# Layer 0 of a four-layer graph network: one excursion from the weighing per tile, and its weights fetched during the first product

## The chip, the core and the metric

The kernel runs on one core of a Trainium2 chip. The core has a matmul engine (TensorE, PE in the profile; its weight loads are listed as PEld), three elementwise engines (VectorE or DVE, ScalarE or ACT, GpSimd or POOL) and queues that issue DMA transfers (SyncE, SP, issues nearly all of them here). The engines run side by side, each in the order of its own instruction stream, and wait for each other through semaphores. The metric is the device time of one execution in microseconds; lower is better.

## The reference

Four graph layers, each followed by a residual sum and a layer norm. x is 8 x 2048 x 64 in float32, adj is 2048 x 2048, sparse and row-normalised. Layer 0 is the one that the change touches, with the beginning of layer 1:

```python
# layer 0: node-wise weights from a 16-wide embedding, three graph terms
w = einsum('nd,dkio->nkio', embedding, weight)      # d = 16, k = 3
b = einsum('nd,do->no', embedding, bias)
As = [I, A, 2 * A @ A - I]
x_g = einsum('knm,bmc->bnkc', stack(As), x)
out = einsum('bnki,nkio->bno', x_g, w) + b
x = layernorm(x + out)
# layer 1, first lines
h = x @ W
s = leaky_relu(h @ a_node, 0.2)
alpha = softmax(where(H.T > 0, s, NEG))             # 64 hyperedges
agg = einsum('ben,bnf->bef', alpha, h)
beta = sigmoid(h @ a_gn + agg @ a_ge)
industry = einsum('nm,bmf->bnf', adj / deg, x @ W_ind)
...
```

Layers 1 (the rest), 2 and 3 use adj again as a matrix product each.

## The kernel before, in words

The 2048 nodes are cut into 16 tiles of 128; j counts them. A tile's data are 128 nodes by 512 columns (8 batches times 64 channels). adj is turned into a mask of zeros and ones and a factor for each row (s1), so that products with it can be done as two exact halves in a fast matmul type: every operand of such a product is split into a high and a low part (y_hi, y_lo).

**First product** (`first_product`, lines 444 to 544). y1 = A x for all tiles, in 32 pieces of the adjacency, with the membership lists of layer 1 prepared between the matmuls (`prepare`, `memberships`). Its accumulators come from a pool of seven (`ps_acc`).

**Layer 0's loop** (`layer0`, lines 987 to 1403). The loop at line 1337 goes over j from 0 to 16. For each tile it does eight *weighings* (`weigh`, g = 0 to 7). A weighing multiplies the three terms of the tile (x, y1 and y2, transposed) with a slice of the layer's weights on PE, on two halves of 64 rows, into a buffer pp (`ps_p`, two buffers of two banks); VectorE then drains it with four operations that scale by the embedding and add to r (L1141). All other work is placed by hand between the weighings, by the value of g: `normed` (layer norm of tile j-1, in three steps), `first_terms` (transposing y1 of tile j+1, its bias through a small matmul bp, and starting r with x plus bias), `project` (h = x W and x W_ind of tile j-2), `product` (y2 of tile j+1, 32 matmuls), `to_features` (transposing the normed tile), `compare` (checks that the mask times its factor is adj), `scaled` (mask times factor and the column sums for the degrees, on GpSimd), `mask` (mask of tile j+2), `scores` (eight matmuls with `wa` for the attention logits, exponential), `low_part` and `gather` (the weighted sum over hyperedges, `aggp`), `second_term` (transposing y2) and `degrees`.

PE leaves the weighing four times in a tile: after g = 2 (`first_terms`), 3 (`project`, `product`, `to_features`), 6 (`second_term`, `scores`, `gather`) and 7 (`degrees`); each of these lines stands below. `program_order` (line 212) fixes the order of PE, VectorE, ScalarE and GpSimd to that of the program text. SP is not fixed: a scheduler places its transfers by priority and by what they wait for. The buffers of the loop are tiles of one large pool (`own`), shared in turn by the table `homes`, and small ones in `l0s`, whose storage was used before by the lists' preparation. `load_w0` is called after the first product; `load_weights` (layer 1's small weights, and the sums for `wa`) in the first round of the loop.

Of the kernel before, what the change touches and what calls it, by code (L numbers as in the profile page):

```python
# [18 lines left out]
P = 128  # L19
# [43 lines left out]
def kernel(  # L63
# [170 lines left out]
    def load_w0(pool):  # L234
        w_sb = pool.tile([P, K, D * C], F32, tag="w", name="w0_sb")
        for h in range(2):
            nc.sync.dma_start(w_sb[h * 64:(h + 1) * 64], w0)
        emb_sb = pool.tile([P, NT, D], F32, tag="emb", name="emb_sb")
        nc.sync.dma_start(emb_sb, emb.rearrange("(t p) d -> p t d", p=P))
        bias_sb = pool.tile([D, C], F32, tag="bias", name="bias0_sb")  # L240
        nc.sync.dma_start(bias_sb, bias0)
        return w_sb, emb_sb, bias_sb
# [201 lines left out]
    def first_product(own, pre, rawp, mskp, y_hi, y_lo, prepare, after):  # L444

        x_hi, x_lo = buffer(own, 0, "x_hi"), buffer(own, 1, "x_lo")
        with tc.tile_pool(name="acc0", bufs=7, space=PSUM) as ps_acc, tc.tile_pool(
# [18 lines left out]

            steps = prepare(ps_s)
# [37 lines left out]
            with program_order():  # L505
# [5 lines left out]
                for n, (q, i, kk, h) in enumerate(pieces):  # L511
                    begin(n + 2)
                    if i + h == 0:
                        accs[q] = [
                            ps_acc.tile([P, BC], F32, tag="acc", name=f"y1p_{4 * q + jj}")
                            for jj in range(4)
                        ]
                    m = m_of.pop(n)
# [468 lines left out]
    def layer0(  # L987
        own, l0s, rawp, mskp, ps_acc, ps_tr, ps_p, w_sb, emb_sb, bias_sb, bad, deg, y_hi, y_lo,
        layer1s, load_weights, late_weights, begun,
# [4 lines left out]
        h_sb, wb, wa, vecs, av_sb, pm, es, hgr, aggp, rden, early = layer1s  # L994
        (raws, msk), terms, resid, norm, srow = begun, {}, {}, {}, {}
        x1s, xTs, hps, hss, mds = {}, {}, {}, {}, {}

        homes = {"xT": (0, 1, 2), "xs": (3, 4), "hs": (5,), "hsf": (15,), "y1T": (6, 7), "r": (8, 9),
# [15 lines left out]
        def load_x(j):  # L1014
            ncols = slice(j * P, (j + 1) * P)
            xT = tile("xT", f"xT_{j}", (P, NP, P))
            nc.sync.dma_start(xT, xt[:, :, ncols])
            et = tile("et", f"et_{j}", (D, P))
            nc.sync.dma_start(et, embt[:, ncols])
            xs = tile("xs", f"xs_{j}")  # L1020
            nc.sync.dma_start(xs, xn[ncols, :])
            terms[j] = {"x": xT, "et": et, "xs": xs}
# [29 lines left out]

        def first_terms(j):

            tr = ps_tr.tile([P, NP, P], F32, tag="tr", name=f"try1_{j}")
            if j > 1:
                y1 = tile("y1", f"y1_{j}", bufs=1)
                nc.gpsimd.tensor_tensor(y1, y_hi[:, j, :], y_lo[:, j, :], ALU.add)
            for pr in range(NP):
                pc = slice(pr * P, (pr + 1) * P)  # L1060
                if j > 1:
                    transpose(tr[:, pr, :], y1[:, pc])
                    continue
# [9 lines left out]
            bp = ps_tr.tile([P, QW], F32, tag="tr", name=f"bp_{j}")  # L1073
            nc.tensor.matmul(bp[:, 0:C], terms[j]["et"], bias_sb, start=True, stop=True)
            bn = tile("bn", f"bn_{j}", (P, C))
            nc.scalar.copy(bn, bp[:, 0:C])
            r = tile("r", f"r0_{j}")
            for bq in range(2):
                nc.gpsimd.tensor_tensor(  # L1079
                    r[:, 4 * bq * C:4 * (bq + 1) * C]  # L1080
                    .rearrange("p (h l c) -> p h l c", h=2, l=2),
                    swapped(terms[j]["xs"], bq),
                    bn.rearrange("p (h l c) -> p h l c", h=1, l=1).to_broadcast([P, 2, 2, C]),
                    ALU.add,
                )
            resid[j] = r
# [58 lines left out]
        def normed(j, step):  # L1145
            r = resid[j]
            if step == 0:
                s = tile("s", f"s_l0_{j}", (P, B))
# [7 lines left out]
            elif step == 1:  # L1156
                var = tile("var", f"var_l0_{j}", (P, B))
# [8 lines left out]
                std = tile("std", f"std_l0_{j}", (P, B))  # L1166
# [27 lines left out]
        def scores(j):  # L1194
            sp = ps_tr.tile([P, NP, 2, 2], F32, tag="tr", name=f"sgp_{j}")
            for pr in range(NP):
                nc.tensor.matmul(
                    sp[:, pr].rearrange("p i h -> p (i h)"), xTs[j][:, pr, :],
                    wa.rearrange("p i h -> p (i h)"), start=True, stop=True,
                )  # L1200
            sg = tile("sg", f"sg_{j}", (P, NP, 2))
            nc.scalar.copy(sg, sp[:, :, 0, :])
            nc.scalar.copy(hgr[:, j, 0, :].rearrange("p (r h) -> p r h", h=2), sp[:, :, 1, :])
            ej = es[:, j, :]
            nc.vector.scalar_tensor_tensor(
                ej.rearrange("p (r h) -> p r h", h=2), sg, 0.2, sg, op0=ALU.mult, op1=ALU.max
            )
            nc.vector.tensor_scalar(ej, ej, TOP, None, op0=ALU.min)
            nc.scalar.activation(ej, ej, AF.Exp)

        def project(j, h_first=False):

            mm = ps_p.tile([P, 2, 2, 4 * C], F32, tag="pp", name=f"hp_{j}")
            mm = mm.rearrange("p h l (m x) -> p h (l m) x", m=2)
            for pr in range(NP):
                for h in range(2):
                    rs = slice(h * 64, (h + 1) * 64)
                    nc.tensor.matmul(
                        mm[:, h, pr, :], xTs[j][rs, pr, :], wb[rs], start=True, stop=True
                    )  # L1220
            if j not in mds:
                md = tile("md", f"md_{j}", (P, 2, E))
                nc.gpsimd.tensor_copy(r_(md), pm[:, j, :].unsqueeze(1).to_broadcast([P, 2, E]))
                mds[j] = md.rearrange("p h e -> p (h e)")

            def by_half(t):
                return t.rearrange("p (r h c) -> p h r c", h=2, c=C)


            stay = j >= len(kept_i)  # L1230
            if stay:
                hi, lo = y_hi[:, j, :], y_lo[:, j, :]
            else:
                hi, lo = (tile(k, f"{k}_{j}", bufs=1) for k in ("ihi", "ilo"))
# [6 lines left out]
            if not stay:  # L1241
                for t, kept_part in zip((hi, lo), kept_i[j]):
# [8 lines left out]
            hss[j] = tile("hs", f"hs_hi_{j}"), hs  # L1251
            nc.scalar.copy(r_(hss[j][0]), hs)

        def low_part(j):
            if j < NT - 1:
                hi, hs = hss[j]

                lo = tile("x1", f"hs_lo_{j}", bufs=1)
                nc.gpsimd.tensor_tensor(r_(lo), hs, hi, ALU.subtract)
                hss[j] = hi, lo  # L1260
# [63 lines left out]
        load_x(0)  # L1324
        load_adj(1)
        load_x(1)
        with program_order():
            for j in range(2):
                for h in range(2):
                    mask(j, h)  # L1330
            first_terms(0)
            scaled(0, 0)
            scaled(0, 1)
            for _ in product(0):
                pass
            second_term(0)
            for j in range(NT + 1):
                first = j == 0
                if not first:
                    when(j + 2, load_adj)  # L1340
                when(j + 2, load_x)
                for g in range(8):
                    when(j, weigh, g)
                    if g == 0:
                        if j == NT:
                            spread()
                        when(j - 1, normed, 0)
                        if first:
                            compare(0, 0)
                            compare(0, 1)  # L1350
                            load_adj(2)
                            load_weights()
                        if j == 2:
                            late_weights()
                    elif g == 1:
                        when(j - 1, normed, 1)
                        if j == NT:
                            denp.append(
                                ps_p.tile([P, 2, 2, 4 * C], F32, tag="pp", name="denp")[:, 0, 0, 0:B]
                            )  # L1360
                            denominators(0, NT - 1)
                            early.extend(industry_early())
                            early.pop(0)(5)
                        if first:
                            degrees(0)
                        when(j + 1, scaled, 0)
                    elif g == 2:
                        when(j - 1, normed, 2)
                        when(j + 1, first_terms)
                    elif g == 3:  # L1370
                        when(j - 2, project)
                        if j + 1 < NT:
                            for _ in product(j + 1):
                                pass
                        when(j - 1, to_features)
                        when(j + 1, compare, 0)
                        when(j + 1, scaled, 1)
                        if j == NT - 2:
                            for t in range(len(kept_i)):
                                for y, kept_part in zip((y_hi, y_lo), kept_i[t]):  # L1380
                                    nc.sync.dma_start(y[:, t, :], kept_part)
                        when(j + 2, mask, 0)
                        when(j + 2, mask, 1)
                    elif g == 5:
                        when(j + 1, compare, 1)
                        when(j - 2, low_part)
                        if j:
                            next(flags, None)
                    elif g == 6:
                        when(j + 1, second_term)  # L1390
# [815 lines left out]
```

## Time and profile before

| | us |
|---|---|
| three runs, median | 1308.96 (1307.51 to 1308.96) |
| the profiled execution | 1308.88 |
| its span, first to last instruction | 1307.5 |
| first product, to its last matmul | 0 to 134.97 |
| joint: to the first weighing of tile 1 | 134.97 to 194.16 |
| tiles 1 to 14 | 194.16 to 662.49 |
| tile 15 | 662.49 to 689.16 |
| tail, to the last gather's end | 689.16 to 708.2 |
| the rest: layers 1, 2 and 3 | to 1307.5 |

The inner borders are read from PE's timeline. A profile is one execution recorded by the hardware. Its page gives the busy time of each engine, the span in 40 slices, the DMA queues, the chain of work that ended last, and the costliest groups of instructions; further views give the timeline of an engine, the waits, and busy times in chosen stretches. In a timeline the columns are start, duration, engine, line, operation, output and inputs, shapes and count; in brackets stands the idle time before an instruction and what ended it. A matmul of full float32 appears as two passes, so a count of x4 means two matmuls. Matmuls are pipelined and overlap, so on PE the distance between starts is the real cost, not the duration.

### The profile page before, as it was taken

What the parts mean: (1) busy time and instruction counts of PE and PEld (TensorE: products, weight loads), DVE (VectorE), ACT (ScalarE), POOL (GpSimd) and SP (SyncE); (2) the same over time, 40 slices, a digit from 0 to 9 for tenths busy, and PEclk for the clock granted to TensorE, in tenths of its full rate; (3) what the DMA queues carried; (4) which work ended last, traced back from release to release, by engine and by line L of the source; (5) the groups of instructions that cost most, each with busy time, mean ns of one, the idle gap of its engine ahead of it and who ended that gap; (6) DMA issues with size and microseconds to landing.
All of it is one profiled execution on the core that took longest, in us unless ns stands there. A gap on an engine that the chain in (4) does not pass through costs nothing. (4 is left out here: it accounts for less than half of the span.)

```text
span 1307.5 us, 20046 instructions
## 1 busy us (share of the span) xinstructions
PE 1250.4 (96%) x7724; PEld 1005.3 (77%) x7724; DVE 887.6 (68%) x1597; ACT 378.0 (29%) x852; POOL 512.2 (39%) x419
## 2 busy tenths in 40 slices
PE   9999789999999999999998599999998899999996
PEld 8887568888888888888886377777766788888885
DVE  5555368888887777778674567777774666655544
ACT  3000101222222222222222356666665521111111
POOL 1000354555555555555411568888872600000000
PEclk9999889999999999999998599999998999999998
DMA  8889532333332333332352212222220233334551
GB/s 285 253 234 182 162 116 93 108 104 103 107 102 97 108 108 108 108 108 81 121 179 97 80 65 97 97 98 97 81 97 1 82 112 129 107 119 153 184 177 67
DMA packets 100951, 157.22 MB, mean 120 GB/s; under 512 B 12912, under 2 KB 64496, under 8 KB 94832
## 3 DMA queue, kind: packets, MB, share of 16 engines
q1 hardware_dynamic: 98368, 151.65, 35.7%
q10 hardware_dynamic: 2304, 4.20, 0.8%
q8 instruction: 63, 1.03, 0.3%
q0 software_dynamic: 176, 0.02, 0.1%
q14 instruction: 40, 0.33, 0.1%
HBM read 118.08 MB, written 37.76 MB: 119 GB/s over the span
## 5 line engine op out<-in xcount | busy, mean ns | idle before, releaser
L1141 DVE SCALAR_TENSOR_TENSOR r<-pp,emb_sb,r 128x256 f32<-128x256 f32 x512 | 247.3, 483 | 109.1 <-PE pp L1130 94.0
L1130 PE MATMUL pp<-w_sb,xT 64*128 64x256 f32 x1024 | 161.6, 392 | 6.5 <-DVE r L1141 6.5
L1130 PE MATMUL pp<-w_sb,y1T 64*128 64x256 f32 x1024 | 154.1, 377 | 0.0
L1130 PE MATMUL pp<-w_sb,y2T 64*128 64x256 f32 x1024 | 154.1, 377 | 0.0
L1079 POOL TENSOR_TENSOR r<-xs,bn 128x256 f32<-128x256 f32 x32 | 22.8, 732 | 244.6 <-issue 216.8
L1130 PEld LDWEIGHTS pp<-w_sb,xT 64*128 64x128 f32 x1024 | 95.0, 187 | 24.6 <-issue 9.6
L1130 PEld LDWEIGHTS pp<-w_sb,y1T 64*128 64x128 f32 x1024 | 100.3, 188 | 11.0
L1130 PEld LDWEIGHTS pp<-w_sb,y2T 64*128 64x128 f32 x1024 | 100.1, 188 | 10.9
L1093 PE MATMUL y2p<-y_hi,msk 128*128 128x512 f32 x256 | 103.7, 405 | 0.0
L523 PE MATMUL y1p<-x_hi,m 128*128 128x512 f32 x256 | 103.0, 402 | 0.1
L1093 PE MATMUL y2p<-y_lo,msk 128*128 128x512 f32 x256 | 101.9, 398 | 0.0
L1468 PE MATMUL ind<-y_hi,mj_l 128*128 128x512 f32 x240 | 101.7, 424 | 0.0
L523 PE MATMUL y1p<-x_lo,m 128*128 128x512 f32 x256 | 101.0, 395 | 0.0
L1468 PE MATMUL a<-v_hi,mj_l 128*128 128x512 f32 x256 | 100.1, 392 | 0.0
L1468 PE MATMUL a<-v_lo,mj_l 128*128 128x512 f32 x256 | 100.0, 391 | 0.0
L1468 PE MATMUL a<-y_lo,mj_l 128*128 128x512 f32 x240 | 95.1, 396 | 0.0
L1468 PE MATMUL a<-y_hi,mj_l 128*128 128x512 f32 x240 | 94.9, 395 | 0.0
L1468 PE MATMUL ind<-y_lo,mj_l 128*128 128x512 f32 x240 | 94.6, 394 | 0.0
L1032 POOL TENSOR_TENSOR ms<-msk,srow 128x1024 f32<-128x1024 f32 x32 | 90.3, 2821 | 10.0 <-DVE ms L1048 5.7
L770 POOL TENSOR_TENSOR ez<-ez,coef 128x1024 f32<-128x1024 f32 x32 | 69.9, 2184 | 56.2 <-DVE ez L768 54.3
L440 DVE TENSOR_SCALAR msk<-adj 128x1024 fp32r<-128x1024 f32 x32 | 61.9, 1971 | 1.1 <-DMA adj<-in_at 1.1
L745 DVE TENSOR_TENSOR gp<-gp,rest 128x1024 f32<-128x1024 f32 (+1 forms) x32 | 30.9, 966 | 45.3 <-PE gp L738 45.0
(289 smaller groups left out, 2455.5 us busy)
## 6 DMA issues: line engine op xcount, KB each, us to landing
mj_l<-mask SPq DMA_DIRECT2D x46, 1024.0 KB, 4.9
adj<-in_at SPq DMA_DIRECT2D x64, 256.0 KB, 3.9
mask<-msk SPq DMA_DIRECT2D x32, 512.0 KB, 4.6
raw<-in_at SPq DMA_DIRECT2D x31, 512.0 KB, 5.2
oh<-oh SPq DMA_DIRECT2D x32, 128.0 KB, 3.9
xT<-in_xt SPq DMA_DIRECT2D x16, 256.0 KB, 3.0
xs<-in_xn SPq DMA_DIRECT2D x16, 256.0 KB, 2.9
kept<-x SPq DMA_DIRECT2D x16, 256.0 KB, 2.0
```

The source lines that it names most:

```text
L440: nc.vector.tensor_scalar(r_(m), raw, 0.0, None, op0=ALU.is_gt)
L523: nc.tensor.matmul(accs[q][jj], r_(m[:, t, jj * P:(jj + 1) * P]), r_(part[:, mt, :]), start=i + h + t == 0 and part is x_hi, stop=i == 3 a ...
L745: nc.vector.tensor_tensor(by_b(gp[:, 0:n]), by_b(gp[:, 0:n]), per_b(rest, 2 * i, n), ALU.mult)
L770: nc.gpsimd.tensor_tensor(by_b(ez), by_b(ez), per_b(coef, 2 * i, 2), ALU.mult)
L1032: nc.gpsimd.tensor_tensor(ms, m, srow[j].unsqueeze(1).to_broadcast([P, 8, P]), ALU.mult)
L1079: nc.gpsimd.tensor_tensor(r[:, 4 * bq * C:4 * (bq + 1) * C] .rearrange("p (h l c) -> p h l c", h=2, l=2), swapped(terms[j]["xs"], bq), bn. ...
L1093: nc.tensor.matmul(acc, r_(msk[j, mt // 8][:, mt % 8, :]), r_(part[:, mt, :]), start=mt == 0 and part is y_hi, stop=mt == NT - 1 and part ...
L1130: nc.tensor.matmul(pp[:, h, pl, :], terms[j][name][rs, 2 * bq + pl], w_sb[rs, k, dq * 4 * C:(dq + 1) * 4 * C], start=k == 0, stop=k == K - 1,)
L1141: nc.vector.scalar_tensor_tensor(rb, ppv[:, :, dd, :], emb_sb[:, j, d:d + 1], rb, op0=ALU.mult, op1=ALU.add)
L1468: nc.tensor.matmul(acc, r_(a[:, mt, :]), r_(part[:, mt, :]), start=mt == 0 and part is hi, stop=mt == NT - 1 and part is lo,)
```

## The change

Layer 0's loop is put in another order, and some of its pieces are cut differently.

- PE leaves the weighing once in a tile, after g = 4, in a new function `visit`. It holds, in this order: the second half of the projection of tile j-2 and its attention weights, the last step of the norm of j-1, a comparison, `first_terms` of j+1, hs of j-2, the product of j+1, the masks of j+2, the second comparison, the transposes of j-1, the gather of j-2, `second_term` and `degrees` of j+1, and the first half of the projection of j-1. VectorE's other work moves there too, except the first two steps of the norm (after g = 0 and 2) and the steps of `flags` (g = 6).
- `scores` and `wa` are gone. Two columns are added to `wb`, so that a projection of 130 columns gives the logits as well; the projection is done in two halves, each in its own pp buffer. The sums for the two columns (`score_weights`) are made after g = 5 of tile 0.
- The bias of all nodes is computed in the first product (`node_bias`, 16 small matmuls, after its first piece) from four tiles `et` that lie in the storage of the last four y_lo tiles, and kept in `bn_all`; the tile-wise bp is gone.
- `load_w0` returns a function `fetch`; that and `load_weights` are called at piece 16 of the first product.
- On GpSimd the masks of a tile are scaled after g = 5 and the next g = 0, the sum y_hi + y_lo is made after g = 0 (`first_sum`), and r is begun after g = 5 (`begin_sum`). xs has one buffer instead of two.

The core of the diff:

```diff
+        def visit(j):
+            if j < NT:
+                when(j - 2, project, 1)
+                when(j - 2, weights_of)
+            when(j - 1, normed, 2)
+            when(j + 1, compare, 0)
+            when(j + 1, first_terms)
+            if j < NT:
+                when(j - 2, weighted)
+            if j + 1 < NT:
+                for _ in product(j + 1):
+                    pass
+            when(j + 2, mask, 0)
+            when(j + 2, mask, 1)
+            when(j + 1, compare, 1)
+            when(j - 1, to_features)
...
+            when(j - 2, gather)
+            when(j + 1, second_term)
+            when(j + 1, degrees)
+            when(j - 1, project, 0, j == NT)
...
+            begin_sum(0)
+            load_xs(1)
             first_terms(0)
             scaled(0, 0)
             scaled(0, 1)
             for _ in product(0):
                 pass
+            compare(0, 0)
+            compare(0, 1)
             second_term(0)
+            degrees(0)
+            scaled(1, 0)
             for j in range(NT + 1):
...
                     if g == 0:
...
                         when(j - 1, normed, 0)
+                        when(j + 1, scaled, 1)
+                        when(j + 1, first_sum)
-                    elif g == 1:
+                    elif g == 2:
                         when(j - 1, normed, 1)
...
+                    elif g == 4:
+                        visit(j)
                     elif g == 5:
+                        if j == 0:
+                            score_weights()
+                        when(j + 2, scaled, 0)
+                        when(j + 1, begin_sum)
+                        when(j + 2, load_xs)
...
+                    elif g == 6 and j:
+                        next(flags, None)
+                        if j == NT - 1:
+                            project(NT - 2, 1)
+                            weights_of(NT - 2)
+                            weighted(NT - 2)
```
```diff
+        def project(j, n, h_first=False):
+            mm = ps_p.tile([P, 2, 2, 4 * C], F32, tag="pp", name=f"hp_{j}_{n}")
...
+            for r in range(2):
                 for h in range(2):
                     rs = slice(h * 64, (h + 1) * 64)
                     nc.tensor.matmul(
-                        mm[:, h, pr, :], xTs[j][rs, pr, :], wb[rs], start=True, stop=True
-                    )
+                        mm[:, h, r, :], xTs[j][rs, 2 * n + r, :], wb[rs], start=True, stop=True
+                    )
...
+            nc.scalar.copy(by_batch(sgs[j]), mm[:, :, :, 2 * C])
+            nc.scalar.copy(by_batch(hgr[:, j, 0, :]), mm[:, :, :, 2 * C + 1])
```
```diff
+            def node_bias():
...
+                    bp = ps_acc.tile([P, NT // 2, C], F32, tag="acc", name=f"bp_{half}")
+                    for t in range(NT // 2):
+                        j = half * (NT // 2) + t
+                        nc.tensor.matmul(
+                            bp[:, t, :], et[j // 4][0:D, (j % 4) * P:(j % 4 + 1) * P], b0,
+                            start=True, stop=True,
+                        )
...
+                    if n == 1:
+                        node_bias()
+                    elif n == 2:
+                        keep_bias()
+                    elif n == 16:
+                        midway()
```

## The prediction

> **What bounds the kernel now.** I read the page first (busy shares and the clock row), then the busy time by stretch, then the timeline of layer 0's loop engine by engine, then the joint between the first product and layer 0.
>
> ```profile
> PE 1250.4 (96%) x7724; PEld 1005.3 (77%) x7724; DVE 887.6 (68%) x1597; ACT 378.0 (29%) x852; POOL 512.2 (39%) x419
> PEclk9999889999999999999998599999998999999998
> ```
> ```profile
> 390.00:620.00 230.00, 229.87 (x1815) 194.01 (x1817) 183.03 (x329) 52.92 (x105) 120.05 (x102) 1.00 0.31 103
> 620.00:700.00 80.00, 76.62 (x626) 65.38 (x622) 54.44 (x123) 17.59 (x35) 23.38 (x24) 0.98 0.39 129
> ```
> The columns of the second fence are stretch, length, then busy time on PE, PEld, DVE, ACT, POOL, the granted clock, DMA share, GB/s. In mid-loop PE is busy for 229.87 of 230 us at full clock while VectorE has a fifth of its time free: the loop lasts as long as PE's instruction stream, and only what shortens that stream, or makes it wait, moves the time. The stream itself has seams:
>
> ```profile
> 456.14 0.60 PE L1130 MATMUL pp<-w_sb,y2T 64*128 64x256 f32 x4
> 456.67 0.66 PE L167 MATMUL try<-ident,y 128*128 128x128 f32 x4
> 457.16 0.95 PE L1197 MATMUL sgp<-wa,xT 128*128 128x4 f32 x8
> 457.97 0.48 PE L1266 MATMUL aggp<-hs_hi,md 128*128 128x512 f32 x1
> 458.29 0.40 PE L1266 MATMUL aggp<-hs_lo,md 128*128 128x512 f32 x1
> 458.62 0.70 PE L1130 MATMUL pp<-w_sb,xT 64*128 64x256 f32 x4
> 459.15 0.60 PE L1130 MATMUL pp<-w_sb,y1T 64*128 64x256 f32 x4
> 459.58 0.60 PE L1130 MATMUL pp<-w_sb,y2T 64*128 64x256 f32 x4
> ```
> First column: start. Inside the weighing (64-row tiles) one row follows the next after 0.43 us. Leaving it for full-height matmuls takes 0.53 (456.14 to 456.67), and so does the first row after the return (458.62 to 459.15). An excursion thus costs 0.1 us going out and 0.1 to 0.2 coming back beyond its contents, and there are four in each tile, after the third, fourth, sixth and eighth weighing. A tile lasts 33.47 us (product starts 440.73 and 474.20).
>
> ```profile
> 464.51 2.04 DVE L1141 SCALAR_TENSOR_TENSOR r<-pp,emb_sb,r 128x256 f32<-128x256 f32 x4 [0.95 <-PE pp L1130]
> 466.48 0.67 DVE L1149 TENSOR_REDUCE s_l<-r 128x8 f32<-128x512 f32 x1
> 467.18 0.69 DVE L1150 SCALAR_TENSOR_TENSOR r<-s_l,r 128x512 f32<-128x512 f32 x1
> 467.79 2.04 DVE L1141 SCALAR_TENSOR_TENSOR r<-pp,emb_sb,r 128x256 f32<-128x256 f32 x4
> ```
> VectorE drains one weighing (four operations, 1.97 us from start to next) in less than PE makes one (six rows, 2.59), 0.31 after its end. With two pp buffers it may fall 0.3 us behind before PE waits.
>
> ```profile
> 143.63 0.65 PE L1074 MATMUL bp<-bias_sb,et 16*128 16x64 f32 x2 [5.40 <-DMA et<-in_embt]
> 144.22 0.80 PE L1093 MATMUL y2p<-y_hi,msk 128*128 128x512 f32 x1
> ...
> 170.49 1.23 PE L1130 MATMUL pp<-w_sb,xT 64*128 64x256 f32 x4 [4.70 <-DVE r L1141]
> ```
> ```profile
> 140.56 0.33 SPq L1012 DMA_DIRECT2D srow<-s_row  x1
> ```
> The joint has two waits: 5.40 us for tile 0's embedding, 4.70 us for VectorE.
>
> **What the skill says.** The Trainium skill, "TensorEngine Tiling (Array Packing)", Key Properties, says that changing the tiling mode drains TensorE; the 0.1 us at each seam agrees. "TensorE: Matmul & The Clock Gate", Part 1, has the clock halve after an idle window of about 3.4 us and recover after a busy one; here idle stretches of 5.4 and 4.7 us are followed by half-rate rows until 149.9 and 174.1, while 2.16 us (to 137.13) is not. "GPSIMD Engine Reference", Key points, has GpSimd share its SBUF interfaces with VectorE instructions of a two-port mode or two SBUF inputs; here the 64x64 product of L1439 lasts 2.37 us beside a GpSimd operation and 0.25 alone, and a mask of L440, 0.68 alone, has a median of 2.33 in mid-loop.
>
> **The change, part by part**, against the profiled execution (1308.88 us, span 1307.5; the median of the runs is 1308.96, so no correction).
>
> *Weights of layer 0 fetched at step 16.* The two w_sb fetches are already issued at 47.0 and 68.7 and the embedding at 99.7, and the instruction order of the changed kernel has them in nearly the same places of SP's queue: 0. The eight small fetches of load_weights, and w2's, move ahead of some adjacency pieces; PE waits for no such piece in the first product now (its only waits there, 3.0 us in all, are at start and for the lists' VectorE chain). 0, at most 1.
>
> *Biases of all nodes in the first product.* 16 small matmuls of two passes, 0.11 us each by the spacing of the L1066 rows: 32 x 0.11 + 0.2 for two seams = 3.7 us on PE, which has no gap there. Bounds 2 and 5. The seven accumulators now come round one sooner to the second quarter: up to 0.3, inside the bound.
>
> *The joint.* The wait for et goes, and the product of tile 0 runs at 141 to 149 at full clock. But dgp(0) now stands before weighing 0 on PE, and needs GpSimd's masks scaled and summed. These start when srow lands. Its issue waits for storage of the lists' last stores: 140.56 now, 144.3 with the 3.7 added; landing takes 2.8, so 147.1. GpSimd's chain (two of ms 2.4, cs 1.3, 0.73, 0.46, then 0.46) is 10.3: weighing 0 begins at about 157.6, against 155.96 now, and after 7 us of idling runs its first 4 to 6 us at half rate (2.3 lost). Tile 0 then needs 20.7 of weighing and 10.0 of visit. After its sixth weighing come score_weights, 4.9 us on VectorE (163.19 to 168.15 now, wherever GpSimd works beside it): weighing 6 is drained late and tile 1 starts 4.1 later, plus 1.0 of clock. 157.6 + 2.3 + 20.7 + 10.0 + 5.1 = 195.7, against 194.16. The late item thus changes from et to srow and GpSimd; first product and joint together +1.5. Bounds -6 and +5.
>
> *The loop, tiles 1 to 14.* Now 194.16 to 662.49, 468.3 us. After: 8 weighings x 2.59 = 20.7. The visit: half a projection 0.49 (16 rows of hp take 0.98), seam 0.1, four transposes three times 0.43, product 7.44, gather 0.56, degree 0.15, half a projection 0.49 with seam 0.1: 10.6. The eight score matmuls (0.81) are gone, two columns of 130 in their place (0.01); bp (0.36 with its seam) is gone; three of four round trips. In the visit trx covers y2's copy, and the copy of xT1 after it (0.69 + 0.58 on ScalarE) is late by 0.2. Against that, no excursion follows weighing 2 any more, so the centring after weighing 0 (1.31 on VectorE) shows: draining weighing 1 ends 0.4 after PE could begin weighing 3. Period 20.7 + 10.8 + 0.4 = 31.9. Thirteen tiles of it, and tile 1 without gather and first half at 30.9: 445.6, so -22.7.
> The rest I cost at nothing because the product hides it, 7.4 us long: VectorE from the visit's start V drains weighing 4 until 2.3, low part and weights to 3.1, norm to 4.2 (trx needs it at 8.5), comparison 5.6, masks and comparison to 9.2 alone or 11.6 at the contended 2.3 per mask; weighing 5 asks for it at 13.5. The weights: exponential 3.3, hs on GpSimd 4.4, copy 5.1, low part 6.4, gather asks at 8.9. GpSimd's scaling then runs to about V + 22, due at 32. On SP, xs waits for begin_sum with the next adjacency halves behind it: issued by V + 15, due at V + 37.
>
> *Tile 15.* There is no product in its visit, so the same chain stands bare: gather 13 waits until V + 6.4, the projection until about 7.5, for 2.1 of work. 20.7 + 0.4 + 7.5 + 0.5 (its extra projection) + 1.5 (clock) = 30.6 against 26.7 (662.49 to 689.16): +3.9. Bounds +1, +6.
>
> *The tail.* From the last weighing to the last gather is now 19.0 us (689.16 to 708.2); it contains tile 14's projection (696.69) and a wait of 2.92 for xT behind it. Without them: norm at +7.9 as now, transposes and copy 9.2, two half projections with four ScalarE copies each to 12.2, weights 13.2, hs 14.3, gather 15.3: -3.7. Bounds -6, 0.
>
> Sum: 3.7 - 2.2 (joint by itself) - 22.7 + 3.9 - 3.7 = -21.0. 1308.9 - 21.0 = 1288.
>
> **Rivals.**
> *A, the visit waits.* The chain through the exponential and GpSimd, or masks at their longest (2.88), reaches gather or weighing 5 late by about 1 us in each tile. For it: GpSimd and VectorE do meet there. Against: 2.5 and 1.9 us of room. Saving per tile falls to 0.5: -22.7 becomes -8, total near 1302.
> *B, slower: VectorE's block becomes the bound.* All its side work now sits in one stretch before weighing 5's drain instead of being spread over the tile. Room is 1.9 us at contended masks; each microsecond beyond it costs 14. It takes away the whole gain once the block is about 3.4 us longer than I have it, so masks near 4 us, and at 4.5 gives 1288 + 14 x (4.4 - 1.9) = 1323. Against: the longest mask now is 2.88, and GpSimd has less to do in the visit than now.
> *C, the fetch does nothing* because the scheduler had done it already: taken as true above, and worth 0 either way.
>
> **How the numbers follow.** Forecast 0.73, A 0.13, B 0.12, and 0.02 for a loop that gains nothing yet stalls nowhere. The forecast's own range joins period 31.4 to 32.4 (-30 to -16) with the ends: 1277 to 1298. To leave out no more than 2 in 10 it is stretched over A: 1277 to 1303. Differences under 0.2% (2.6 us) can't be told from none. Faster is the forecast and most of A, 0.85; same 0.04 (the last case and A's upper end); slower 0.11.
>
> **What would show it.** Product starts 31.9 apart; one seam out and one back per tile; a PE wait on VectorE of 0.3 to 0.4 at weighing 3; a GpSimd wait on srow and an idle PE near 150 to 157; a wait of some 4 us at tile 1's start; 6 us of gaps in tile 15. I'd be wrong if PE waits in mid-loop on hs_lo or on weighing 5's drain, or if the joint is several microseconds off.

## The result, and the profile after

The changed kernel takes 1308.98 us (median of 20 runs, 1305.62 to 1313.6), the kernel before in the same runs 1308.85 (1307.16 to 1313.43). The ratio is 0.9999, with a 95% interval of 0.9991 to 1.0007: no change that can be measured. Forecast were 1288 and a gain.

The page of the changed kernel, its row of busy times and its clock row:

```profile
PE 1227.7 (94%) x7596; PEld 1003.4 (77%) x7596; DVE 899.2 (69%) x1613; ACT 379.2 (29%) x900; POOL 506.4 (39%) x419
...
PEclk9989989999999999999988699999998999999998
```

PE has 22.7 us less to do than before (1250.4), and the span is only 1.9 us shorter. So the removed work is removed; idle time has come in its place. A new dip in the clock row, in the third slice (65 to 98 us), lies in the first product; the dip at the joint was there before. The stretches between the same borders as before, with the columns stretch, length, busy time on PE, PEld, DVE, ACT, POOL, granted clock, DMA share and GB/s:

```profile
0.00:149.55 149.55, 138.54 (x616) 112.75 (x616) 73.72 (x177) 20.08 (x34) 9.37 (x19) 0.97 0.81 219
149.55:206.75 57.20, 43.13 (x283) 35.95 (x283) 30.82 (x56) 3.94 (x8) 35.48 (x30) 0.88 0.39 129
206.75:656.51 449.76, 442.85 (x3562) 390.45 (x3564) 384.20 (x706) 105.45 (x246) 225.64 (x199) 1.00 0.33 111
656.51:689.96 33.45, 27.03 (x226) 23.78 (x222) 20.56 (x45) 6.83 (x20) 3.67 (x5) 0.90 0.37 111
689.96:707.70 17.74, 14.11 (x77) 11.05 (x76) 7.05 (x21) 2.90 (x11) 6.16 (x7) 0.82 0.29 92
707.70:1305.60 597.90, 562.08 (x2841) 429.37 (x2839) 382.81 (x610) 239.98 (x582) 226.10 (x160) 0.96 0.29 104
```

Set against the lengths before and the forecast (all in us):

| stretch | before | after | difference | forecast |
|---|---|---|---|---|
| first product | 134.97 | 149.55 | +14.6 | +3.7 |
| joint | 59.19 | 57.20 | -2.0 | -2.2 |
| tiles 1 to 14 | 468.33 | 449.76 | -18.6 | -22.7 |
| tile 15 | 26.67 | 33.45 | +6.8 | +3.9 |
| tail | 19.04 | 17.74 | -1.3 | -3.7 |
| the rest | 599.30 | 597.90 | -1.4 | 0 |
| sum | 1307.5 | 1305.6 | -1.9 | -21.0 |

The loop did most of what was expected. In mid-loop one tile follows the next after 32.00 us instead of 33.47, with one recorded wait in each (PE's timeline of the kernel before, then of the changed kernel):

```profile
440.73 0.50 PE L1093 MATMUL y2p<-y_hi,msk 128*128 128x512 f32 x1
...
474.20 0.50 PE L1093 MATMUL y2p<-y_hi,msk 128*128 128x512 f32 x1
```
```profile
422.01 0.60 PE L167 MATMUL trx<-ident,x 128*128 128x128 f32 x4
...
440.35 0.70 PE L1167 MATMUL pp<-w_sb,xT 64*128 64x256 f32 x4 [0.40 <-DVE r L1178]
...
454.01 0.60 PE L167 MATMUL trx<-ident,x 128*128 128x128 f32 x4
```

The largest miss stands in the first product. SP's queue there in the changed kernel (start, time that the issue took, queue, line, transfer):

```profile
61.85 0.55 SPq L513 DMA_DIRECT2D raw<-in_at  x1
62.45 0.91 SPq L240 DMA_DIRECT2D w_sb<-in_w  x1
70.83 1.17 SPq L348 DMA_DIRECT2D oh<-oh  x2
72.05 0.61 SPq L430 DMA_DIRECT2D S<-S  x1
72.77 0.46 SPq L380 DMA_DIRECT2D pT<-pT  x1
73.68 0.64 SPq L241 DMA_DIRECT2D emb_sb<-in_emb  x1
74.38 1.53 SPq L1474 DMA_DIRECT2D wb<-in_w  x1
...
79.45 0.43 SPq L1478 DMA_DIRECT2D av_sb<-in_av  x1
79.98 2.56 SPq L348 DMA_DIRECT2D oh<-oh  x4
82.64 1.21 SPq L356 DMA_DIRECT2D pT_raw<-in_hypt  x2
83.89 2.01 SPq L513 DMA_DIRECT2D raw<-in_at  x4
```

Between 61.85 and 83.89 no piece of the adjacency is issued. In the kernel before, the next piece went out at 62.98, ahead of the list store that SP waits for, and VectorE made its mask at 74.25 (SP's queue and VectorE's timeline of the kernel before):

```profile
62.98 0.91 SPq L485 DMA_DIRECT2D raw<-in_at  x2
65.84 1.18 SPq L342 DMA_DIRECT2D oh<-oh  x2
```
```profile
74.25 0.68 DVE L488 TENSOR_SCALAR m<-raw 128x1024 fp32r<-128x1024 f32 x1
```

In the changed kernel that store (70.83) stands ahead of the piece. VectorE makes the piece's mask, and PE needs the mask; the two timelines of the changed kernel, VectorE's and then PE's:

```profile
88.45 0.69 DVE L516 TENSOR_SCALAR m<-raw 128x1024 fp32r<-128x1024 f32 x1 [9.11 <-DMA raw<-in_at]
```
```profile
89.52 0.42 PE L403 MATMUL sm<-tri,pT 128*128 128x64 f32 x1 [7.42 <-DVE oh L426]
89.75 0.77 PE L557 MATMUL y1p<-x_hi,m 128*128 128x512 f32 x1
90.33 0.63 PE L557 MATMUL y1p<-x_lo,m 128*128 128x512 f32 x1
90.75 0.63 PE L557 MATMUL y1p<-x_hi,m 128*128 128x512 f32 x1
```

PE stands still for 7.42 us. The profile blames a list operation (oh), but that one stands behind the mask on VectorE, which had waited 9.11 us for the transfer. Afterwards PE's rows follow each other 0.43 us apart instead of 0.23, for nine rows: another 1.9 us.

### The profile page after: what moved, and what is told of

It reads as the page before. It is cut to its first block, busy times and chain, and to the rows that moved or that the text cites. A ratio compares the mean times of both kernels' runs of the same rounds, so it can differ in the third digit from the quotient of the medians.

```text
span 1305.6 us, 19815 instructions
## 1 busy us (share of the span) xinstructions
PE 1227.7 (94%) x7596; PEld 1003.4 (77%) x7596; DVE 899.2 (69%) x1613; ACT 379.2 (29%) x900; POOL 506.4 (39%) x419
## 3 DMA queue, kind: packets, MB, share of 16 engines
q8 instruction: 62, 1.02, 0.3%
## 4 chain that ended last, share of the span: by engine, by line
PE 79%; DVE 9%; issue 5%; ACT 2%; POOL 2%; DMA 2%; SPq 1%; DVEq 0%; ACTq 0%; POOLq 0%
PE pp L1167 20%; PE a L1527 18%; PE ind L1527 9%; PE y2p L1130 8%; PE y1p L557 5%; DVE r L1178 5%; PE fc L872 3%; PE df L881 2%; PE gp L772 1%; PE yp L1627 1%; PE try L167 1%; PE hp L1247 1%; PE trm L167 1%; PE red L813 1%; PE dp L792 1%
## 5 line engine op out<-in xcount | busy, mean ns | idle before, releaser
L1167 PE MATMUL pp<-w_sb,xT 64*128 64x256 f32 x1024 | 159.4, 383 | 10.3 <-DVE r L1178 8.6
L1167 PE MATMUL pp<-w_sb,y1T 64*128 64x256 f32 x1024 | 156.9, 378 | 0.0
L1167 PE MATMUL pp<-w_sb,y2T 64*128 64x256 f32 x1024 | 156.8, 378 | 0.0
L1167 PEld LDWEIGHTS pp<-w_sb,xT 64*128 64x128 f32 x1024 | 100.9, 189 | 24.5 <-PE pp L1167 12.9
L1167 PEld LDWEIGHTS pp<-w_sb,y1T 64*128 64x128 f32 x1024 | 104.7, 188 | 7.6
L1167 PEld LDWEIGHTS pp<-w_sb,y2T 64*128 64x128 f32 x1024 | 104.6, 188 | 7.4
L1286 POOL TENSOR_TENSOR hs<-h,es 128x512 f32<-128x512 f32 x16 | 18.0, 1126 | 218.2 <-ACT es L1274 218.2
L1066 POOL TENSOR_TENSOR ms<-msk,srow 128x1024 f32<-128x1024 f32 x32 | 81.2, 2536 | 47.6 <-DVE msk L446 36.6
L1082 DVE SCALAR_TENSOR_TENSOR ms<-ms,adj 128x1024 f32<-128x1024 f32 x32 | 72.6, 2272 | 7.8 <-POOL ms L1066 7.8
L1191 ACT ACTIVATE sq_l<-r 128x512 f32<-128x512 f32 x16 | 10.1, 631 | 204.0 <-DVE r L1187 204.0
```

What stands on the lines that cost most here:

```text
L1066: nc.gpsimd.tensor_tensor(ms, m, srow[j].unsqueeze(1).to_broadcast([P, 8, P]), ALU.mult)
L1082: nc.vector.scalar_tensor_tensor(ms, ms, 1.0, raws[j][h], op0=ALU.mult, op1=ALU.not_equal, accum_out=bad[:, 2 * j + h:2 * j + h + 1],)
L1167: nc.tensor.matmul(pp[:, h, pl, :], terms[j][name][rs, 2 * bq + pl], w_sb[rs, k, dq * 4 * C:(dq + 1) * 4 * C], start=k == 0, stop=k == K - 1,)
L1286: nc.gpsimd.tensor_tensor(b_view(hs), b_view(h_sb[:, j, :]), bcast(es[:, j, :]), ALU.mult)
```

## The experiments

Unless said otherwise every kernel is timed in five rounds beside the kernel before on the same chip. Ratios are to the kernel before, with 95% intervals; where two experiments are set against each other, it is by their ratios, since they did not all run on the same chip. A difference of two such ratios carries some 3 to 4 us of uncertainty. The theory after the reading above, called Q in the expectations: the eight small fetches of `load_weights`, together with what they push ahead of them, hold up the pieces in SP's queue. Its rivals are N, the node biases, and D, the bytes on the DMA engines.

**1. The small fetches back in the loop.** Only `load_weights` leaves step 16:

```diff
-                    lambda: (fetch(), load_weights()),
+                    lambda: (fetch(), ),
...
-                    score_weights, late_weights, begun,
+                    (load_weights, score_weights), late_weights, begun,
...
+                        if j == 0:
+                            score_weights[0]()
...
-                            score_weights()
+                            score_weights[1]()
```

> The changed kernel, with only the eight small fetches of load_weights put back where the kernel before has them (after tile 0's first weighing); the large fetch stays at step 16. Theory Q (the queue: the pieces of adjacency from step 19 on stand behind these fetches on SP, VectorE and then PE run dry): 9 to 12 us below the changed kernel's 1309, so 1297 to 1300; no VectorE wait of 9 us on a raw piece; the first transposes of layer 0 start near 141 instead of 151.7. Theory N (the node biases in the first product cost the 14.6 us, by their matmuls and by the accumulators that they turn round): within 3 us of 1309, transposes not before 148. Theory D (the bytes of the weights take the DMA engines from the pieces, wherever they are queued): some 3 to 6 us below 1309, since later they meet the same pieces' stores.

1298.6 us, ratio 0.9911 (0.9889 to 0.9933). The first transposes of layer 0 start at 142.14 instead of 151.71. SP's queue in this run, and VectorE's one wait for a piece there:

```profile
62.52 0.50 SPq L240 DMA_DIRECT2D w_sb<-in_w  x1
70.87 1.17 SPq L348 DMA_DIRECT2D oh<-oh  x2
...
73.70 0.57 SPq L241 DMA_DIRECT2D emb_sb<-in_emb  x1
74.33 2.00 SPq L513 DMA_DIRECT2D raw<-in_at  x2
```
```profile
79.68 0.69 DVE L516 TENSOR_SCALAR m<-raw 128x1024 fp32r<-128x1024 f32 x1 [0.30 <-DMA raw<-in_at]
```

This run measures the slack of the queue. The piece goes out at 74.33, 11.4 us later than in the kernel before, and VectorE waits 0.30. Of the 11.4, 5.0 are no delay, since VectorE comes to this point 5.0 us later too (its mask before this one is made at 76.27 instead of 71.24); the other 6.3 were slack, used up to the last. The kernel before shows the same: the piece goes out at 62.98, takes about 5 us to land (74.33 to 79.68 here), and its mask is made at 74.25, so some 6 us are to spare. The changed kernel issues it at 83.89, another 9.56 us later, and VectorE waits 9.11. Of the 9.56, 5.6 are the eight fetches (74.38 to 79.98) and 3.9 the next list's stores and load, which now stand ahead of the piece as well.

**2. The same change made to the kernel before.** Its `load_w0` is split in the same way, and both calls are put at step 16; nothing else:

```diff
+                    if n == 16:
+                        midway()
                     m = m_of.pop(n)
```

> The kernel before, with the fetch of layer 0's weights and the eight small ones put at step 16 of the first product, and nothing else of the change. Theory Q: 8 to 12 us slower than before (1317 to 1321), with VectorE waiting some 9 us for a raw piece near 85 and PE's first transposes near 147. Theory N: within 1 us of before. Theory D: 3 to 6 us slower.

1322.5 us, ratio 1.0092 (1.0066 to 1.0117), so 12.1 us slower. PE idles 5.98 us at 84.74 and its first transposes begin at 146.53 (137.13 before). The fetch alone costs what the rest of the change gains. Q holds on both sides, and N, which has no part in this kernel, is out as the main cause of the miss.

**3. The small fetches on ScalarE's queue**, at the same step, `nc.scalar.dma_start` for `nc.sync.dma_start`:

> The changed kernel with the eight small fetches issued at the same step 16, by ScalarE's queue instead of SP's. Theory Q: SP is freed of 5.5 us of issuing ahead of the pieces, so at least half of the loss comes back: 1298 to 1304. Theory D: no change, 1307 to 1311, the same bytes at the same time. Theory N: no change either.

1301.8 us, ratio 0.9927 (0.9902 to 0.9951): most of the loss comes back with the same bytes at nearly the same time (issued from 76.39 to 80.66). D falls as the main cause. The order in SP's queue is that of the first experiment. One wait of VectorE for a later piece is left in the profile (3.70 us, at 92.42); its cause stays open.

**4. The small fetches at step 16, the large one late.** The opposite of the first experiment:

```diff
-                    lambda: (fetch(), load_weights()),
+                    lambda: (load_weights(), ),
...
+            fetch()
             h_sb = buffer(own, 1, "h")
```

> The changed kernel with the large fetch (layer 0's weights and the embedding) put behind the first product in the program and the eight small fetches left at step 16. If it is the place in SP's queue that costs (theory Q), the built order tells the time: here the small fetches come to stand before the list stores of the first quarter, where three pieces are in hand, and pieces 19 to 21 stand ahead of the second list's store as in the kernel before; 1298 to 1303. If it is the number of the fetches issued during the first product, wherever: 1305 or more.

1300.6 us, ratio 0.9917 (0.9901 to 0.9933). The scheduler places seven of the small fetches at 52.22 to 55.87, where pieces are in hand, and the pieces stay ahead of the list store as in the kernel before. So the same eight fetches in the first product cost 11 us in one place of the queue and nothing measurable in another.

Four runs belong together here: ratio 0.9911 with only the large fetch at step 16, 0.9917 with only the small ones, 0.9937 with neither (the second kernel of experiment 5), 0.9999 with both. Neither costs anything measurable by itself; both together cost about 11 us. Wherever the large fetch stands at step 16 (the changed kernel, experiments 1 to 3), its second half and the list store that SP waits for are issued ahead of the piece, and that uses up the slack. Where it comes late, the piece goes out ahead of that store (at 63.80 here, at 61.82 in the other kernel). The small fetches cost only on top of that.

**5. The biases.** Two kernels with both fetches behind the first product, one with the biases and one without them (no fetch of the transposed embedding, no matmuls, zeros as the sum, so that the bias term of layer 0 is left out):

> As the run with the small fetches late, and with the large fetch after the first product in the program too; the node biases are left out (no fetch of the embedding's transpose, no 16 matmuls, no copies; their sum is filled with zeros), so the output lacks the bias term of layer 0. Theory Q: 2 to 5 us below the run with the fetches late (forecast of the biases' cost 3.7). Theory N: 10 us or more below the run with the fetches late, which itself stays near 1309.

> The changed kernel with both fetches behind the first product, the biases in place: the twin of the run without biases, whose queue it shares. If the biases cost their matmuls alone (3.7, as forecast): 1297.5 to 1299. If the half rate that follows them in the records of some runs (a mean clock of 0.93 to 0.97 over the first 50 us) is part of their price: 4 to 7 us above the run without biases, 1298 to 1301, and in the profile PE's rows go 0.43 apart behind them. If they cost nothing because PE would wait there anyway: 1294 to 1296.

Without: 1294.3 us, ratio 0.9878 (0.9854 to 0.9902). With: 1300.4, ratio 0.9937 (0.9923 to 0.9951). Joining the two intervals, the biases cost 0.59%, give or take 0.28: 4 to 11 us. The two profiled executions are closer, 3.6 us apart at the first transposes (142.24 and 138.64). PE's timeline with the biases:

```profile
11.61 3.78 PE L481 MATMUL bp<-bn_all,et 16*128 16x64 f32 x32
15.32 0.50 PE L557 MATMUL y1p<-x_hi,m 128*128 128x512 f32 x1
15.66 0.40 PE L557 MATMUL y1p<-x_lo,m 128*128 128x512 f32 x1
...
16.35 0.61 PE L557 MATMUL y1p<-x_hi,m 128*128 128x512 f32 x1
16.76 0.63 PE L557 MATMUL y1p<-x_lo,m 128*128 128x512 f32 x1
```

The matmuls take 3.7 us (11.61 to 15.32), the forecast figure. Then, from 16.35, eight rows take 3.4 us instead of 1.8 (0.43 apart, not 0.23): 1.6 us more that the sum did not have.

**6. The joint.** On the kernel of the first experiment, the second comparison of tile 0 and its degree matmul move from ahead of weighing 0 to behind weighing 4:

```diff
             compare(0, 0)
-            compare(0, 1)
             second_term(0)
-            degrees(0)
...
                     elif g == 4:
+                        if j == 0:
+                            compare(0, 1)
+                            degrees(0)
                         visit(j)
```

> On the kernel with the small fetches late (1298.6): the second comparison of tile 0 and its degree matmul are moved from ahead of weighing 0 to behind weighing 4. If the joint is held by the degree matmul waiting for GpSimd's sums and by the half rate that the idle stretch leaves behind, as the prediction has it: weighing 0 begins near 155 instead of 161.7 and at full rate, 6 to 9 us less, 1290 to 1293. Rival: the joint is held by y2's transposes behind VectorE's first comparison, so that nothing is gained beyond 1 to 2 us.

1297.5 us, ratio 0.9903 (0.9885 to 0.9921): 1 us, within what can't be told from none. Weighing 0 does begin 9.8 us earlier (151.90 instead of 161.70), so the forecast place was right; but it stops after two rows for y2's transposes on VectorE (2.27 us) and goes on at half rate. Behind the visit of tile 0 the run is still 6.0 us ahead (181.07 against 187.03). Most of that is given back at the first weighing of tile 1 (the expectation of a later run calls it weighing 7 of tile 0). VectorE's timeline, and PE's:

```profile
187.40 2.05 DVE L1488 TENSOR_TENSOR prod<-wb,vecs 64x64 f32<-64x64 f32 x1
...
189.73 0.93 DVE L1488 TENSOR_TENSOR prod<-wb,vecs 64x64 f32<-64x64 f32 x1
```
```profile
193.09 1.23 PE L1167 MATMUL pp<-w_sb,xT 64*128 64x256 f32 x4 [3.98 <-issue]
```

The eight operations of `score_weights` last 5.0 us here (185.94 to 190.95), beside GpSimd's scaling; in the first experiment they lasted 2.7, and PE waited 1.65 at this place. PE's wait is put down to "issue", but it ends when the drain behind these operations has freed a buffer.

**7. Tile 15.** On the kernel of the first experiment, in tile 15 alone `to_features`, `gather` and the first half projection stand after g = 5 instead of 4, tile 14's second half projection after g = 7 instead of 6, and `spread` at its start:

```diff
                         when(j + 2, load_xs)
+                        if j == NT - 1:
+                            to_features(NT - 2)
+                            gather(NT - 3)
+                            project(NT - 2, 0)
...
-                        if j == NT:
+                        if j == NT - 1:
                             spread()
```

> On the kernel with the small fetches late: in tile 15 alone, the transposes of tile 14, the gather of 13 and the half projection stand one weighing later, the other half projection of tile 14 behind the last weighing, and the mask copies for the denominators are made at the start of tile 15. If tile 15's 6.7 us over the kernel before are its bare chain (2.93 + 0.75 + 0.56 of waits, then half rate, then 1.79 and 1.63): 5 to 8 us less, 1291 to 1294. Rival: the chain of the last tile through the normalisation is what ends last and the fillers are only moved: within 2 us of 1298.6.

1295.8 us, ratio 0.99 (0.9883 to 0.9916): 1.4 us against the first experiment, which is the rival's forecast and not the 5 to 8 us. PE's timelines of the changed kernel in tile 15, and of this run at its end:

```profile
673.77 0.44 PE L167 MATMUL trx<-ident,x 128*128 128x128 f32 x2 [2.93 <-DVE x L1214]
674.96 0.69 PE L167 MATMUL trx<-ident,x 128*128 128x128 f32 x2 [0.75 <-DVE x L1214]
...
676.67 0.80 PE L1301 MATMUL aggp<-hs_lo,md 128*128 128x512 f32 x1 [0.56 <-POOL hs_lo L1294]
...
687.29 0.70 PE L1167 MATMUL pp<-w_sb,xT 64*128 64x256 f32 x4 [1.79 <-DVE r L1178]
...
691.78 3.55 PE L1318 MATMUL denp<-es,md 128*128 128x8 f32 x28 [1.63 <-POOL md L1310]
```
```profile
673.75 3.29 PE L1318 MATMUL denp<-es,md 128*128 128x8 f32 x28
...
683.38 1.11 PE L167 MATMUL trx<-ident,x 128*128 128x128 f32 x4 [3.94 <-DVE x L1214]
```

In place of these four waits inside tile 15 there are now two, 1.85 (for a drain, at 662.84) and 0.31, and denp starts without one. Tile 15 lasts 26.4 us instead of 33.4 (646.74 to 673.18). But the last tile's norm ends as a chain of its own: PE then waits 3.94 us for it and goes on at half rate, and the tail lasts 21.8 us instead of 17.7.

**8. The centring split.** On the kernel of the first experiment the sum stays after g = 0, and the subtraction with the squares goes after g = 1:

```diff
                 nc.vector.tensor_reduce(s, b_view(r), AX.X, ALU.add)
+                norm[j] = s
+            elif step == 0.5:
+                s = norm[j]
                 nc.vector.scalar_tensor_tensor(
...
+                    elif g == 1:
+                        if j < NT:
+                            when(j - 1, normed, 0.5)
```

> On the kernel with the small fetches late: the sum for the centring stays behind weighing 0, the centring itself goes behind weighing 1. If PE's 0.40 at weighing 3 of each tile is VectorE's 1.31 put in one place, as the prediction has it, the wait vanishes: period 31.6, 15 x 0.4 = 6 us less, 1292 to 1294. Rival: the 0.40 is only moved one weighing on (the centring then meets the variance): within 1 us of 1298.6.

1292.7 us, ratio 0.9873 (0.9856 to 0.9889), 5 us below the first experiment. PE's waits in mid-loop are gone (three, of 0.88, 0.59 and 0.60 us, stay in tiles 4 to 6), and the period is 31.33 (PE's timeline of this run):

```profile
411.52 0.60 PE L167 MATMUL trx<-ident,x 128*128 128x128 f32 x4
...
442.85 0.60 PE L167 MATMUL trx<-ident,x 128*128 128x128 f32 x4
```

That is 0.67 less for each tile, where the records of the wait said 0.40. The changed kernel's rows around such a wait tell why:

```profile
663.92 0.63 PE L1167 MATMUL pp<-w_sb,y2T 64*128 64x256 f32 x4
664.94 0.70 PE L1167 MATMUL pp<-w_sb,xT 64*128 64x256 f32 x4 [0.39 <-DVE r L1178]
665.45 0.63 PE L1167 MATMUL pp<-w_sb,y1T 64*128 64x256 f32 x4
```

The starts are 1.02 and 0.51 apart instead of 0.43 and 0.43: 0.67. The idle time in brackets is counted from the modelled end of the row before, which overlaps the next row when they run on.

**9. Together.** The three edits at once; then with both fetches late and `score_weights` moved ahead of the first comparison in the joint, where VectorE waits for GpSimd; then with nine steps of the industry product behind the last weighing instead of five.

```diff
-                            score_weights[1]()
...
+            score_weights[1]()
             compare(0, 0)
             second_term(0)
...
-                            early.pop(0)(5)
+                            early.pop(0)(9)
```

> The three edits together on the kernel with the small fetches late. If they are independent stretches, their gains add: 1278 to 1284. If the last tile's end is the same chain in all of them, the gain of the tile-15 edit is lost: 1284 to 1288.

> The three edits together (1288.8 before this), with both fetches late, and the score columns' eight VectorE operations moved from behind weighing 5 of tile 0 to the joint, where VectorE waits 4.6 us for GpSimd. If these operations, stretched to 5.0 us beside GpSimd, took back what the joint's edit gained: the wait of 3.98 at weighing 7 of tile 0 goes with the half-rate rows behind it, 4 to 5 us less, 1283 to 1285. Rival: weighing 7 then waits for something else, or the operations meet GpSimd in the joint and push the first weighing back: within 1.5 us of 1288.8.

> As the run before, with nine steps of the industry product behind the last weighing instead of five, taken from those that come later. If the 3.9 us of idle PE ahead of the last transposes only costs by the half-rate rows that follow it (transposes, gather, projection): 1 to 2 us less. Rival: the four steps are missing as fillers later, no change.

1288.8 us, ratio 0.9831 (0.9813 to 0.9849); 1282.1, ratio 0.9776 (0.9752 to 0.9801); 1281.5, ratio 0.9782 (0.9766 to 0.9797). The first is 10.5 us below the first experiment by the ratios, where the single gains make 7.4, which is the same within the uncertainty; its median is just above both ranges of the expectation. The second is 0.55% lower, more than the joint's edit gave by itself: the eight operations last 1.9 us at their new place (151.63 to 153.58), where GpSimd is idle, and in its profile tile 1 begins without a wait, so that the earlier weighing 0 is kept. This run also has the large fetch late; its share was not measured by itself here, but late or early made no clear difference above (0.9937 and 0.9911). The third can't be told from the second. In its profile the transposes run at full rate, but other waits of about a microsecond come up behind them. The last two beat both kernels, by 2.2%. Shortening the last norm's chain, and computing the biases in PE's idle time at the joint, were not tried.

## Why the prediction was wrong, point by point

**The fetch: the step that failed.** The prediction saw the order ("the eight small fetches of load_weights, and w2's, move ahead of some adjacency pieces") and priced it "0, at most 1", because "PE waits for no such piece in the first product now". It cost 11 to 12 us (experiments 1 and 2), as much as the rest of the change gained. A wait that is absent says nothing of how near it is. The slack could have been read from the kernel before: issued at 62.98, 5 us to land, needed at 74.25, so 6 us. The piece was put off by 21, or by 16 against VectorE's own delay of 5; 6 of these were free, and the other 10 are about what VectorE waited (9.11). The prediction also named only the fetches, and not the stores that move ahead with them, nor SP's wait for the first of these. And its "0" for the large fetch was a misreading: "nearly the same places of SP's queue" did not hold for the second half of w_sb, which came to stand, with that store, ahead of the piece and took all the slack. Rival C, with the fetch worth 0 "either way", rested on the same step. The rest of the miss is smaller and of another kind: tiles 1 to 14, tile 15 and the tail together gained 9.4 us less than forecast.

**The biases.** 3.7 was right for the matmuls. The half rate behind them (1.7 us in this profile) was missing, and the bound of 5 was a little low. In the changed kernel's first product 7.4 (idle), 1.9 (half rate after it), 3.7 and 1.7 make 14.7 where 14.6 were measured; smaller differences cancel.

**The joint.** -2.0 against -2.2, but by luck: two misses offset each other. Weighing 0 began 22.7 us behind the end of the first product instead of 18.9, since GpSimd's chain started 1.9 us later than forecast and took 12.1 us instead of 10.3 (159.80 to 171.91). From there to tile 1 it took 34.5 us instead of 38.1; the wait at tile 1's start was 1.63 instead of 4.1. That the late item would change from et to GpSimd, with the half rate behind it, was right. The product of tile 0 did not run all at full clock, as forecast: its first rows are at half rate in this profile (153.82 to 155.10), behind a PE wait of the same 2.16 us that had been harmless in the kernel before. Experiment 6 shows what the prediction had only counted once: behind that item stands the next one, `score_weights`.

**Tiles 1 to 14.** The mechanism was right and the size near: -18.6 against -22.7. The period without a wait is 31.33 (31.5 forecast), and the wait costs 0.67 (0.4 forecast); for 14 tiles the two make 1.4 us. The rest is in the early tiles. `flags` was not priced at all: its steps now stand behind weighing 6, close ahead of the centring, and the longest is a reduction of 1.94 us. VectorE's and PE's timelines of the changed kernel:

```profile
301.98 1.94 DVE L265 TENSOR_REDUCE flagbox<-pm 128x64 f32<-128x1024 f32 x1
```
```profile
306.02 0.70 PE L1167 MATMUL pp<-w_sb,xT 64*128 64x256 f32 x4 [0.87 <-DVE r L1178]
```

Tiles 4 to 6 have such a wait each (0.87, 0.63, 0.60). Rivals A and B did not happen: PE waits in mid-loop neither for hs_lo nor behind VectorE's block.

**Tile 15 and the tail.** +6.8 against +3.9, and -1.3 against -3.7. The bare chain in the visit was forecast (7.5 us for it; it takes 8.2, from 670.20 to 678.42), and so was the half rate behind it. Not forecast were two waits of PE that come from where the pieces stand: the half projection of tile 14 takes a pp buffer after weighing 6, so that weighing 7 waits 1.79, and in the tail denp waits 1.63 for GpSimd's mask copies. Experiment 7 shows that removing them gains little, since the last norm's chain ends last.

## What to carry to other kernels

Before a transfer is moved ahead of others in a queue, work out for each one behind it when it will be issued and when it is needed: an engine that never waits for them now can be a few microseconds from doing so (here 6), and then pays one for one. Two moves that are each free can cost when made together, because both draw on the same slack. Count all that moves along, above all entries that themselves wait for another engine. Where an edit frees time ahead of an order made by hand, look for the next late item on every engine before counting the gain.

## What the runs showed of the hardware

Issuing a DMA on SP takes time that matters: behind the first, the small fetches follow each other 0.47 to 0.64 us apart in the changed kernel's queue (75.96, 76.59, 77.23, 77.87, 78.50, 78.97, 79.45). The Trainium skill, "DMA: Bandwidth & Descriptors", section "Issuing engines are not separate DMA queues", says that issuing from several engines saves only the time to initiate a DMA, "which is usually small relative to the DMA itself". Here this time counted, with all that stood behind it in the queue: moving eight issues to ScalarE's queue brought back 7 us by the medians and 9 by the ratios.

PE's rate halved behind a stretch in which PE was recorded as busy. Behind or during the 32 passes of 16-row matmuls (3.7 us, or 4.2 to 4.9 where the clock falls while they run), the mean clock between 12 and 24 us was 0.72 in three of the eleven profiles with the biases, 0.86 in seven and 1.00 in one; in the three profiles without them it was 1.00. The skill's "TensorE: Matmul & The Clock Gate", Part 1, speaks of idle windows, and of windows that run freely, which fits the change from run to run. Whether it is the few rows of these matmuls that count as idle was not tried. The wait of 2.16 us at the end of the first product shows the same change from run to run: in five of the twelve profiles with the new loop half-rate rows follow it, and from the transposes behind it to the next ones it takes 10.9 to 11.0 us; in seven it takes 9.3.
